# A graph network of four layers on one core: the feed-forward's transpose and the row of f go over DRAM, the relation check to ScalarE

## The chip, the core and the metric

The kernel runs on one core of a Trainium2 chip. Its time is the device time of one execution in microseconds (us). The profile is of one further execution, with its own time.

The engines are PE (TensorE, matrix products; PEld is its loading of weights, which overlaps the products), DVE (VectorE), ACT (ScalarE), POOL (GpSimd) and SP (SyncE, which here only issues transfers). Each engine works through its own list of instructions in order and waits on semaphores for the others. Products go to PSUM, which has eight banks of 2 KB per partition; everything else lies in SBUF, with 128 partitions, or in DRAM.

## The reference: what is computed

There are 64 graphs of 256 nodes with 256 features (x) and a 256 × 256 matrix of integers (adj), all in 32-bit floats. Four layers follow each other, and after each x becomes layernorm(x + layer(x)):

```python
# layer 0: attention with 8 heads where an edge goes one way or the other, then a feed-forward
x1 = layernorm(x + softmax(mask(q @ k.T / sqrt(32))) @ v @ Wo.T + bo)
ff = relu(x1 @ W1.T + b1) @ W2.T + b2
layer0 = layernorm(x1 + ff)
# layers 1 and 2: graph attention ("GAT"), e[i, j] = leaky_relu(f[i] + g[j]) where adj > 0
h = x @ W; f = h @ a[0]; g = h @ a[1]
layer1 = softmax(e) @ h + bias
layer2 = elu(softmax(e) @ h)
# layer 3: two convolutions over the relation adj == 1 (the other relation is always empty here)
conv(h) = elu(h @ w_root + b + (adj == 1).T @ h / degree @ w_rel[1])
layer3 = conv2(conv1(x))
```

In layer 3 both masks are made from the same adj: one is (adj == 1) and (adj != 1), which holds nowhere, so that only one relation is computed. The kernel checks such assumptions as it goes along and keeps the findings (`seen_sum`, `seen_inv`, `seen_fg`, `seen_rel`); a general version of the computation stands behind a branch at the end, and is entered only where one of them does not hold.

## The kernel before, in words

**Graphs.** `graph(g)` (from L653) describes the work on one graph as a list of operations for a planner, each on one engine and with its cost, the tiles that it reads and writes, and a function that issues the instructions. The operations of all 64 graphs go into one plan, so that the engines work on several graphs at a time.

**The order.** `Plan.schedule` (L197) lays all operations out in time before anything is issued: an engine that is free takes, among the operations that are ready and for whose tiles a buffer is free, the one with the earliest due date. The due date is the sum of a date for the kind of operation (`DUE`) and one for the graph (`LATER`). Both are lists of numbers found by a search. `RINGS`, `DRAM` and `SMALL` give the number of buffers of each kind of tile. A transfer has a cost, its time on the issuing queue, and a lag until its data are there (`SENT` 3.2 and `BACK` 5.5 for the bounce described below). An operation with the port mark "uses" is a VectorE operation with which the planner lets no POOL operation marked "waits" overlap. The result is a fixed order on each engine.

**Turning a tile.** A product needs the left operand with the features on the partitions, so each tile of 256 nodes × 256 features is turned before it is multiplied. There are three ways in the kernel:

- `transposed` (L691): four PE transposes (products with the identity) of 128 × 128 into one bank, and a ScalarE copy (L701) to the tile `T`.
- `bounced` (L714): one VectorE instruction turns all blocks of 32 × 32 (L719), four SP transfers write the result, 128 B a piece, to a DRAM tile `rows` (L723), one SP transfer reads it back as `T` (L726). The features come back in another order on the partitions (feature 128k + 32b + c on partition 4c + b), and the weights that are multiplied with them are loaded in that order by `spread` (L594).
- `rearranged` (L704): `bounced` for all but the last five graphs (`QUICK`); for those a ScalarE copy (L709) puts the features in the other order, and `transposed` turns the copy.

The GAT layers and the convolutions use `rearranged`. The feed-forward (L888) uses `transposed` for all graphs, and its W1 lies in plain order; the gain of the layer norm before it is multiplied into W1 at the start (L650, with the column `gcol`), its bias goes through W1 into b1 (L644, with `bcol`). The input of layer 0 has a way of its own (`input_transposed`, L730: eight transfers per graph and one VectorE instruction).

**A GAT layer** (`gat`, L912): four products with the weights give h and, in two more columns, f and g, and VectorE or ScalarE moves them to SBUF. Then f, which lies in one column of h, is needed as a row on every partition. PE makes it with two transposes of a column repeated 128 times, into the bank `pf` (L932). For each half VectorE adds pf, the column of g and the mask (L937); the leaky slope (L940), the exponential on ScalarE (L942) and the products with h (L945) follow.

**The relation** (`relation`, L977): VectorE makes rel = (adj == 1) at L981, and at L982 sums up (adj != 1) × rel, which must be zero, into a column of `seen_rel`.

**At the start** `setup` loads the weights on SP (W1 with one transfer of 1 MB at L602), and POOL loads the rows and columns of biases; `gcol` and `bcol` are two of those loads (L385).

Of the kernel before, what the change touches and what calls it, by code (L numbers as in the profile page):

```python
# [9 lines left out]
F32 = mybir.dt.float32  # L10
# [3 lines left out]
AF = mybir.ActivationFunctionType  # L14
ALU = mybir.AluOpType
# [3 lines left out]
P = 128  # L19
# [8 lines left out]
SENT, BACK = 3.2, 5.5  # L28


RINGS = {"x": 3, "adj": 4, "bits": 2, "am": 2, "gm": 6, "T": 4, "qk": 2, "v": 2, "p": 12, "both": 4, "inv": 1, "ctxT": 2, "X": 8,
         "xr": 1, "hid": 1, "h": 3, "e": 3, "n": 1, "rel": 3, "hi": 2, "lo": 2, "o": 4, "blocks": 1, "turned": 1, "xT": 2}
DRAM = {"rows": 6}
# [1285 lines left out]
```

## Time and profile before

| | |
|---|---|
| three runs | 2799.07 to 2801.94 us, median 2801.02 |
| profiled execution, its own time | 2798.13 us |
| its span | 2796.4 us |
| instructions in the span | 50418 |
| PE busy | 2762.3 us (99%), 16262 products recorded |
| PEld busy | 2128.1 us (76%) |
| DVE busy | 2486.5 us (89%), 6475 instructions |
| ACT busy | 1568.0 us (56%) |
| POOL busy | 855.0 us (31%) |
| moved by DMA | 284.08 MB, mean 102 GB/s |
| DMA packets | 808319, of them 651088 under 512 B |

The span runs from the first to the last recorded instruction, and the device time is 1.7 us longer. A product of 32-bit floats is recorded as two matmuls, a transpose and a product of the relation's type (fp32r) as one. In groups of instructions, a line reads: line of the kernel, engine, operation, output tile <- input tiles, shapes, count, then the busy time in us and the mean duration of one in ns, then how long the engine was idle just before them and what ended that. A line of the code can be that of a helper: all plain products stand under L747. The profile takes matmuls as pipelined, so that the recorded length of one reaches into the next, and the length of one is not the time that it takes from PE. In the transfers, the three figures are the count, the size of one, and the median time from issue to landing in us.

### The profile page before, as it was taken

What the parts mean: (1) busy time and instruction counts of PE and PEld (TensorE: products, weight loads), DVE (VectorE), ACT (ScalarE), POOL (GpSimd) and SP (SyncE); (2) the same over time, 40 slices, a digit from 0 to 9 for tenths busy, and PEclk for the clock granted to TensorE, in tenths of its full rate; (3) what the DMA queues carried; (4) which work ended last, traced back from release to release, by engine and by line L of the source; (5) the groups of instructions that cost most, each with busy time, mean ns of one, the idle gap of its engine ahead of it and who ended that gap; (6) DMA issues with size and microseconds to landing.
All of it is one profiled execution on the core that took longest, in us unless ns stands there. A gap on an engine that the chain in (4) does not pass through costs nothing. (4 is left out here: it accounts for less than half of the span.)

```text
span 2796.4 us, 50418 instructions
## 1 busy us (share of the span) xinstructions
PE 2762.3 (99%) x16262; PEld 2128.1 (76%) x16262; DVE 2486.5 (89%) x6475; ACT 1568.0 (56%) x3753; POOL 855.0 (31%) x1747
## 2 busy tenths in 40 slices
PE   7999999999999999999999999999999999999998
PEld 5787777777777777777777777777777777777774
DVE  5789999898998998998989989989989889899877
ACT  3555565555555555655555555556556555556466
POOL 2223233233232332332332322323323323223232
PEclk9999999999999999999999999999999999999999
DMA  7346455554545555554545556455555545544121
GB/s 188 78 88 125 88 122 104 105 107 103 113 97 107 111 102 102 112 105 102 108 104 110 99 106 118 95 102 113 103 102 110 105 95 108 104 97 103 42 50 32
DMA packets 808319, 284.08 MB, mean 102 GB/s; under 512 B 651088, under 2 KB 769104, under 8 KB 808048
## 3 DMA queue, kind: packets, MB, share of 16 engines
q1 hardware_dynamic: 763680, 229.77, 37.1%
q0 software_dynamic: 44368, 51.01, 12.3%
q8 instruction: 131, 2.15, 0.3%
q14 instruction: 140, 1.15, 0.1%
HBM read 152.19 MB, written 78.64 MB: 83 GB/s over the span
## 5 line engine op out<-in xcount | busy, mean ns | idle before, releaser
L761 POOL TENSOR_SCALAR rstd<-mv 128x2 f32<-128x2 f32 x384 | 116.4, 303 | 1359.4 <-DVE mv L758 1226.0
L747 PE MATMUL bank<-T,w 128*128 128x256 f32 x2048 | 475.4, 380 | 0.1
L747 PE MATMUL bank<-cw,T 128*128 128x512 f32 x1024 | 465.5, 594 | 0.3 <-ACT T L701 0.2
L747 PE MATMUL bank<-w,hid 128*128 128x256 f32 x2048 | 462.3, 379 | 0.0
L768 ACT ACTIVATE X<-X,rstd 128x256 f32<-128x256 f32 x640 | 349.4, 598 | 154.6 <-POOL rstd L764 151.2
L747 PEld LDWEIGHTS bank<-w,hid 128*128 128x128 f32 x2048 | 384.2, 190 | 53.6 <-issue 3.3
L747 PEld LDWEIGHTS bank<-T,w 128*128 128x128 f32 x2048 | 379.9, 190 | 54.8 <-issue 4.8
L847 ACT ACTIVATE p<-bank 128x512 f32<-128x512 f32 x512 | 302.1, 606 | 78.1 <-PE bank L841 78.1
L849 DVE TENSOR_TENSOR p<-p,am 128x512 f32<-128x512 f32 x512 | 331.9, 678 | 7.6 <-ACT p L847 7.4
L747 PEld LDWEIGHTS bank<-cw,T 128*128 128x128 f32 x1024 | 189.1, 190 | 181.0 <-issue 173.5
L762 POOL TENSOR_TENSOR rstd<-rstd,neghalf 128x2 f32<-128x2 f32 x384 | 310.8, 809 | 32.0
L873 DVE RECIPROCAL inv<-bank 128x256 f32<-128x256 f32 x128 | 219.5, 1743 | 110.6 <-PE bank L867 110.6
L902 ACT ACTIVATE hid<-bank,col_b 128x256 f32<-128x256 f32 x512 | 213.5, 468 | 106.9 <-PE bank L747 106.6
L747 PE MATMUL bank<-xT,wqkv 128*128 128x256 f32 x1024 | 238.6, 382 | 14.5 <-DMA wqkv<-in_WqkvT_dram 14.5
L747 PE MATMUL bank<-h,e 128*128 128x259 f32 x1024 | 252.0, 386 | 0.1
L747 PE MATMUL bank<-gw,T 128*128 128x258 f32 x1024 | 246.0, 381 | 0.0
L747 PEld LDWEIGHTS bank<-h,e 128*128 128x128 f32 x1024 | 189.3, 190 | 68.7 <-issue 43.2
L756 DVE BATCH_NORM_STATS2 st<-X 128x6 f32<-128x256 f32 x640 | 237.3, 412 | 4.2
L747 PEld LDWEIGHTS bank<-xT,wqkv 128*128 128x128 f32 x1024 | 193.8, 191 | 44.4 <-DVE row_b L414 14.5
L747 PEld LDWEIGHTS bank<-gw,T 128*128 128x128 f32 x1024 | 189.6, 189 | 29.9 <-issue 3.0
L965 ACT ACTIVATE n<-bank,r 128x256 f32<-128x256 f32 x128 | 60.6, 474 | 239.6 <-DVE X L970 149.2
L999 ACT CAST hi<-bank 128x256 fp32r<-128x256 f32 x256 | 98.7, 386 | 167.1 <-PE bank L747 166.5
(126 smaller groups left out, 4871.5 us busy)
## 6 DMA issues: line engine op xcount, KB each, us to landing
rows<-turned SPq DMA_DIRECT2D x944, 64.0 KB, 2.3
T<-rows SPq DMA_DIRECT2D x236, 256.0 KB, 2.8
adj<-in_adj_dram SPq DMA_DIRECT2D x128, 256.0 KB, 3.5
blocks<-in_x_dram SPq DMA_DIRECT2D x512, 32.0 KB, 2.4
xr<-in_x_dram SPq DMA_DIRECT2D x64, 256.0 KB, 2.9
x<-in_x_dram SPq DMA_DIRECT2D x64, 256.0 KB, 2.9
xr<-row_ln_b POOLq DMA_DIRECT2D x64, 256.0 KB, 5.1
x<-row_bo POOLq DMA_DIRECT2D x64, 256.0 KB, 4.7
```

Of the source, the lines that this page charges most:

```text
L747: nc.tensor.matmul(dst, lhsT=lhs(c), rhs=rhs(c), start=(c == 0), stop=(c == n - 1))
L756: nc.vector.bn_stats(stat()[:, i, :], y()[:, i, :])
L761: nc.gpsimd.tensor_scalar(rstd()[:, 0, :], mv()[:, :, 1], 1.0, EPS, op0=ALU.mult, op1=ALU.add)
L762: nc.gpsimd.tensor_tensor(rstd()[:, 0, :], rstd()[:, 0, :], neghalf[:, 0:NB], op=ALU.pow)
L768: nc.scalar.activation(y()[:, i, :], y()[:, i, :], AF.Identity, bias=rstd()[:, 1, i : i + 1], scale=rstd()[:, 0, i : i + 1])
L847: act(0.58, lambda pr=pr, k=k, sr=s[r]: nc.scalar.activation(pr(), sr(), AF.Exp, accum_out=seen_sum[:, k : k + 1]), [s[r]], [pr])
L849: dve(0.60, lambda pr=pr, kt=kt: nc.vector.tensor_tensor(pr(), pr(), am()[:, kt, None, :].to_broadcast([P, KB, N]), op=ALU.mult), [pr, am] ...
L873: dve(1.62, lambda hg=hg, pc=pc: nc.vector.reciprocal(inv()[:, hg, :], pc()[:, 1, :]), [pc], [(inv, hg)])
L902: act(0.36, lambda f=f, k=k, ph=ph: nc.scalar.activation(hid()[:, f + k, :], ph()[:, k, :], AF.Relu, bias=b1[:, f + k : f + k + 1]), [ph, ...
L965: act(0.36, lambda: nc.scalar.activation(n(), po()[:, 0:D], AF.Exp, scale=r()), [po, r], [n])
L999: act(0.27, lambda i=i, po=po: nc.scalar.copy(hi()[:, i, 0:D], po()[:, D:]), [po], [(hi, i)])
```

## The change

1. The feed-forward turns its tile by `rearranged` in place of `transposed`: over DRAM for 59 graphs, by a ScalarE copy and PE for the last five. W1 is loaded by `spread` with four transfers, and `gcol` and `bcol` by four small transfers each (`cols_spread`), in the same order of features. In products with w1, x1T is read as `xT()[:, kb::KB, :]`, two runs of 128 numbers.
2. `f_on_all` is new: for 59 graphs a VectorE instruction turns the column of f, repeated 32 times, in blocks into `cols`; an SP transfer writes partitions 0, 32, 64 and 96 of it as one row of 256 numbers (1 KB) to DRAM, and a second reads the row to all 128 partitions as `pf`, now a tile in SBUF. The additions of pf get the port mark "uses". The last five graphs keep the PE transposes.
3. The check of the relation becomes a ScalarE instruction: the sum of (rel − 0.5)², which is a quarter for each element that is 0 or 1. At the very end that known sum is subtracted and the rest squared.
4. The rings get `cols` (2), `pf` (3), `row` (6, in DRAM), and `rows` grows from 6 to 8. All numbers of `DUE` and most of `LATER` are new.
5. The general version reloads W1 in plain order and multiplies the gain in again.

```diff
+SENT_ROW, BACK_ROW = 2.6, 4.0
...
-         "xr": 1, "hid": 1, "h": 3, "e": 3, "n": 1, "rel": 3, "hi": 2, "lo": 2, "o": 4, "blocks": 1, "turned": 1, "xT": 2}
-DRAM = {"rows": 6}
+         "xr": 1, "hid": 1, "h": 3, "e": 3, "n": 1, "rel": 3, "hi": 2, "lo": 2, "o": 4, "blocks": 1, "turned": 1, "xT": 2, "cols": 2, "pf": 3}
+DRAM = {"rows": 8, "row": 6}
...
+    def cols_spread(name):
+        w = const.tile([P, KB], F32, tag=f"spread_{name}", name=f"spread_{name}")
+        view = t[name].rearrange("(k b c) -> b c k", b=4, c=32)
+        for b in range(4):
+            nc.gpsimd.dma_start(w[b::4], view[b])
+        return w
...
-    gcol, bcol = cols("ln1_g", KB), cols("ln1_b", KB)
+    gcol, bcol = cols_spread("ln1_g"), cols_spread("ln1_b")
...
-            load(c_w1, w1, "W1T")
+            spread(c_w1, w1, "W1T")
...
-                return xT, lambda kb, i: xT()[:, KB * i + kb, :]
+                return xT, lambda kb, i: xT()[:, kb::KB, :] if i is None else xT()[:, KB * i + kb, :]
...
-                x1T = transposed(x1)
+                x1T, x1T_at = rearranged(x1)
...
-                            lambda kb: x1T()[:, kb, :], KB), [x1T, c_w1], [ph], [hid])
+                            lambda kb: x1T_at(kb, None), KB), [x1T, c_w1], [ph], [hid])
...
+            def f_on_all(h, e):
+                if g < B - QUICK:
+                    cols, row, pf = new("cols", [P, NB, 32]), new("row", [1, NB * P]), new("pf", [P, N])
+                    dve(0.13, lambda: nc.vector.transpose(cols().rearrange("p i c -> p (i c)"),
+                                                          h()[:, :, F_COL : F_COL + 1].to_broadcast([P, NB, 32])),
+                        [(h, 0), (h, 1)], [cols], "uses")
+                    op("SP", 0.45, lambda: nc.sync.dma_start(row().rearrange("o (i b c) -> (o b) i c", i=NB, b=4), cols()[::32]),
+                       [cols], [row], lag=SENT_ROW)
+                    op("SP", 0.45, lambda: nc.sync.dma_start(pf(), row().to_broadcast([P, N])), [row], [pf], lag=BACK_ROW)
+                    return pf, "uses"
...
-                pe("spread", 0.18, spread, [(h, 0), (h, 1)], [pf], [e])
+                pf, port = f_on_all(h, e)
                 for i in range(NB):
                     dve(0.39, lambda i=i: nc.vector.scalar_tensor_tensor(e()[:, i, :], pf(), h()[:, i, G_COL : G_COL + 1],
                                                                          gm()[:, i, :], op0=ALU.add, op1=ALU.min),
-                        [pf, (h, i), gm], [(e, i)])
+                        [pf, (h, i), gm], [(e, i)], port)
...
-                dve(0.60, lambda: nc.vector.scalar_tensor_tensor(
-                    other(), adj(), 1.0, rel().bitcast(F32), op0=ALU.not_equal, op1=ALU.mult,
-                    accum_out=seen_rel[:, g : g + 1]), [adj, rel], [other], "uses")
+                act(0.62, lambda: nc.scalar.activation(other(), rel().bitcast(F32), AF.Square, bias=half[:, 0:1],
+                                                       accum_out=seen_rel[:, g : g + 1]), [rel], [other])
...
+    nc.vector.tensor_scalar(seen_rel, seen_rel, -0.25 * NB * N, None, op0=ALU.add)
+    nc.vector.tensor_tensor(seen_rel, seen_rel, seen_rel, op=ALU.mult)
```

More of the change, by code (lines that the diff above doesn't have):

```diff
@@ L409, in tile_gnn_stack @@
     minus = filled([P, 1], F32, "minus", -1.0)
+    half = filled([P, 1], F32, "half", -0.5)
     neghalf = filled([P, NT], F32, "neghalf", -0.5)
-    gcol, bcol = cols("ln1_g", KB), cols("ln1_b", KB)
+    gcol, bcol = cols_spread("ln1_g"), cols_spread("ln1_b")
     bq = const.tile([P, KB], F32, tag="bq", name="bq")
@@ L711, in rearranged @@
                 xT = transposed(spread)
-                return xT, lambda kb, i: xT()[:, kb, i * P : (i + 1) * P]
+                return xT, lambda kb, i: xT()[:, kb, :] if i is None else xT()[:, kb, i * P : (i + 1) * P]
             def bounced(xt):
@@ L910, in feed_forward, with spread @@
                 return y
+            def f_on_all(h, e):
[8 more added lines that the diff above has]
+                    return pf, "uses"
+                pf = new("bank", [P, N])
+                def spread():
+                    for i in range(NB):
+                        nc.tensor.transpose(pf()[:, i * P : (i + 1) * P],
+                                            h()[:, i, F_COL : F_COL + 1].to_broadcast([P, P]), ident)
+                pe("spread", 0.18, spread, [(h, 0), (h, 1)], [pf], [e])
+                return pf, None
             def gat(xt, layer, gm, seen, bias, finish):
@@ L927, in gat @@
                                                           h()[:, :, F_COL : G_COL + 1], op=ALU.mult), [(h, 0), (h, 1)], [], "uses")
-                pf = new("bank", [P, N])
-                def spread():
-                    for i in range(NB):
-                        nc.tensor.transpose(pf()[:, i * P : (i + 1) * P],
-                                            h()[:, i, F_COL : F_COL + 1].to_broadcast([P, P]), ident)
-                pe("spread", 0.18, spread, [(h, 0), (h, 1)], [pf], [e])
+                pf, port = f_on_all(h, e)
                 for i in range(NB):
@@ L1250, in tile_gnn_stack @@
             nc.vector.tensor_copy(eye[:, h, h * P : (h + 1) * P], ident_b)
+        g_col = gen.sb([P, KB], F32, "g_col")
+        nc.scalar.dma_start(g_col, t["ln1_g"].rearrange("(c p) -> p c", p=P))
+        nc.scalar.dma_start(w1, t["W1T"].rearrange("(c p) n -> p c n", p=P))
+        for c in range(KB):
+            nc.vector.tensor_scalar(w1[:, c, :], w1[:, c, :], g_col[:, c : c + 1], None, op0=ALU.mult)
         w_rel0 = []
```

95 rows, old and new, of tables (DUE, LATER) are left out of this document.

## Prediction

> **What bounds the kernel now.** I read first the table of stretches, which gives each engine's busy time in a stretch of the span (PE, PEld, DVE, ACT, POOL, then granted clock, DMA share, GB/s).
>
> ```profile
> 0.00:50.00 50.00, 31.70 (x233) 25.37 (x233) 24.46 (x57) 14.23 (x38) 16.56 (x29) 0.93 0.79 196
> 50.00:400.00 350.00, 349.94 (x2116) 272.25 (x2116) 306.95 (x773) 191.51 (x474) 101.27 (x208) 1.00 0.50 103
> 400.00:800.00 400.00, 400.00 (x2345) 309.03 (x2345) 366.27 (x951) 226.14 (x547) 126.28 (x249) 1.00 0.53 106
> ...
> 2720.00:2760.00 40.00, 38.06 (x163) 25.39 (x162) 35.76 (x122) 32.59 (x62) 9.10 (x25) 1.00 0.04 8
> 2760.00:2797.00 37.00, 23.00 (x94) 13.12 (x92) 23.07 (x75) 21.42 (x39) 9.52 (x22) 0.86 0.19 52
> ```
>
> From 50 to 2720 us PE has no gap; it idles 18.3 us at the start and some 16 us at the end. But a matmul's recorded duration overlaps the next one, so "busy" alone proves nothing. I therefore took PE's own timeline near the middle, where the first column is the start, the second the length.
>
> ```profile
> 1404.84 3.61 PE L747 MATMUL bank<-w,hid 128*128 128x256 f32 x16
> 1408.29 0.38 PE L932 MATMUL bank<-ident,h 128*128 128x128 f32 x2
> 1408.51 3.62 PE L747 MATMUL bank<-w,hid 128*128 128x256 f32 x16
> ...
> 1424.70 0.61 PE L698 MATMUL bank<-ident,X 128*128 128x128 f32 x4
> 1425.14 5.32 PE L747 MATMUL bank<-cw,T 128*128 128x512 f32 x12
> ```
>
> Sixteen matmuls take 1408.29 − 1404.84 = 3.45 us, 0.216 us from start to start; those of one form are alike all through the middle (the median start-to-start of the 2048 from L747 on w and hid is 0.216, the tenth and ninetieth percentiles 0.215 and 0.216). So PE issues at its own pace and waits for nobody: whatever leaves PE between 50 and 2700 us leaves the span, as long as nothing new makes PE wait. The groups that the change touches (count, then busy us and mean ns):
>
> ```profile
> L719 DVE STREAM_TRANSPOSE turned<-X 128x512 f32<-128x512 f32 x177 | 124.6, 704 | 9.9 <-ACT X L768 7.5 <-ACT hid L902 0.7
> L937 DVE SCALAR_TENSOR_TENSOR e<-bank,h,gm 128x256 f32<-128x256 f32 x256 | 116.2, 470 | 4.6 <-PE bank L932 4.6
> L968 DVE SCALAR_TENSOR_TENSOR n<-n,X 128x256 f32<-128x256 f32 x128 | 52.9, 413 | 2.3 <-ACT n L965 2.3
> L701 ACT COPY T<-bank 128x512 f32<-128x512 f32 x84 | 51.1, 609 | 9.4 <-PE bank L698 9.1
> L932 PE MATMUL bank<-ident,h 128*128 128x128 f32 x256 | 49.0, 273 | 0.0
> L982 DVE SCALAR_TENSOR_TENSOR e<-adj,rel 128x512 f32<-128x512 int32 x64 | 43.6, 681 | 0.1
> L876 ACT ACTIVATE inv<-inv 128x512 f32<-128x512 f32 x64 | 40.3, 630 | 43.6 <-DVE ctxT L874 33.4 <-DVE r L947 4.5
> L698 PE MATMUL bank<-ident,X 128*128 128x128 f32 x256 | 38.8, 274 | 0.0
> ```
>
> **The change, part by part.** *PE.* In 59 of the 64 graphs (all but the QUICK five) the feed-forward loses four transposes, and each of the two GAT layers two. Their price is not their 274 ns but the slot they take: 1425.14 − 1424.70 = 0.44 us for four, 1408.51 − 1408.29 = 0.22 us for two. 59 × 0.44 + 118 × 0.22 = 26.0 + 26.0 = **−52 us**. The last five graphs keep four transposes in the feed-forward, now of a spread copy. [...]
>
> One product is fed differently: the 2048 matmuls with w1 read x1T in two runs of 128 numbers instead of one of 256. No row shows this on that operand. A gain has no ground; the nearest rows are the transposes of L932, which read a column repeated 128 times, and of L698, which read plain columns: 273 and 274 ns, the same slot. I take nothing; the other end is 3% of 1888 × 0.216 us, 12 us, by the spread of the group means of one shape (379 to 391 ns).
>
> *DVE*, busy 2486 us. 59 block transposes × 0.704 = +41.5; the check of the relation goes, 64 × (0.681 + 0.081 for its accumulator) = −48.8. The e addition reads pf from SBUF: between 0.470 (L937, one bank) and 0.413 (L968, SBUF only), 236 × −0.05 = −12, bounds −13 and 0. The new transpose of 64 columns lies between 0.06 (a memset of two columns) and 0.704 (512 columns); 64/512 of 0.704 plus 0.06 is 0.15, nearest to the short one: +18, bounds +7 and +83. Sum −1, bounds −14 and +76: 2485 us of a span near 2750 is 90%, 93% at worst. DVE's waits hide it; the largest is `inv` at L873 waiting 110.6 us for PE. *ACT*, 56% busy: 59 copies × 0.609 = −36, 64 checks × (0.630 + 0.188, L876's row and its accumulator) = +52, five spread copies × 1.107 = +5.5. All beside PE.
>
> *Queues.* SP has some 1000 us of issue work now (944 row writes × 0.63, 512 block loads × 0.45, 236 reads × 0.35, 320 loads and stores × 0.39). It gains 236 × 0.63 + 59 × 0.35 + 236 × 0.45 = 276 us: 37% becomes 47%. The DMA engines stand at 0.53 in the middle; a quarter more bouncing and 118 reads of 128 KB bring at most 0.62. [...]
>
> ```profile
> rows<-turned SPq DMA_DIRECT2D x944, 64.0 KB, 2.3
> T<-rows SPq DMA_DIRECT2D x236, 256.0 KB, 2.8
> ...
> gw<-ga SPq DMA_DIRECT2D x8, 0.5 KB, 1.8
> ```
>
> *The two added waits.* (1) f over DRAM: eviction 0.42 (L923), transpose 0.15, write 1.8 (the 0.5 KB row), read 2.8 (twice its size), two additions 0.94, L940's 0.68, exp 0.63: 7.4 us, 8.0 with the long transpose. I laid the slots of this trace along the PE order of the built changed program. Between a GAT layer's last product and its first product with e stand 11.6 us of other PE work at least and 15.8 at the median (4.7 and 9.2 in the order of before). The cover holds by 3.6 to 8 us. On SP the read of the row waits for its write to land; up to nine transfers stand between the two, in 22 of 118 cases none, and then bounces, loads and the next graph's blocks are held about 1.8 us behind it. On DVE 6 to 31 instructions (median 18) stand between the transpose and the addition that needs pf; behind it wait mostly the multiplications by the mask, and PE's values behind those. (2) The feed-forward over DRAM: addition 0.69, statistics 1.05, POOL 1.6, scaling 1.1, transpose 0.70, four issues 2.5, landing 2.3, read 3.15: 13.1 us, against 23.0 us of PE work at least (median 36.7) between the wo product and w1. Covered.
>
> *The ends.* At the start PE waits until 14.51 for wqkv. In the new SP order one quarter of W1 (256 KB) goes ahead of it; at the 188 GB/s of the first slice that is 1.4 us, plus 0.6 of issue: **+2**. Six more column loads on POOL (0.73 each) fall in its 7.2 us wait for `row_bo`. At the end the last graph's feed-forward needs a spread copy, 1.107 us on its chain: **+1**. Between −1 and +6 for both.
>
> *Sum* against the profiled execution's own time, 2798.1 (span 2796.4 and 1.7 around it): −52 + 3 = 2749. It lies 2.9 below the median of the three runs, so I add 3: **2752**. New due dates also re-order every engine; PE's switches between tilings cost the same table of slots within 2 us (54 instead of 52 us saved over the whole order), left out of the sum.
>
> **The rivals.** *Stalls eat a part.* The PE order has tighter places too: between a conv product and the first product with its rest (lo), 183 pairs have under 2.5 us, against 74 before. For it: PE had no slack waits to lose. Against: pairs under 1.8 us are as many as before (16 and 15). At 0.3 us of stall per graph, or w1 read slower, it gives 2763 to 2790. *Slower.* The row trip through SP in order: where a row's write or read stands behind a bounce that itself waits (SP waited 406.7 us for L756 in 48 times, 9.7 at most), 7.4 us becomes 17. From an average stall of 52/118 = 0.44 us per GAT layer on, nothing is gained; at 1 us the time is 2752 + 118 = 2870. So 2805 to 2870. Against it: the margin above. *It does nothing:* DVE, 91% busy, takes the pace, its waits cannot shrink, and the time stays near 2796. Against: 34 us of its 400 are idle, and the change adds none. *More:* the starts overlap better, under 2741.
>
> **Chances.** 2741 to 2763: 0.72. Partly eaten: 0.14. Same pace by DVE: 0.04. Slower: 0.07. Over 52 us: 0.03. A measurement of this kernel tells about 0.2%, 5.6 us, from no change. Faster 0.72 + 0.14 + 0.03 and half of the DVE case make 0.91, same 0.02, slower 0.07. The range 2741 to 2776 leaves out the larger stalls and the slow case.
>
> **What would show it.** PE: some 15790 matmuls instead of 16262, the transposes of h down to 20, and still 400.00 busy in the middle stretches with more matmuls in each; DVE near 92 to 93% there; ACT's `T` copies 25. Wrong would be: gaps of PE ahead of products with e (f's trip), ahead of w1 (the feed-forward's trip), w1 slots above 0.216, or a start idle well over 20 us.

## The result, and the profile after

The changed kernel takes 2804.55 us at the median (2801.43 to 2812.56) where the kernel before takes 2799.69 on the same chip: a ratio of 1.0019, with a 95% interval of 1.0012 to 1.0026. The forecast was 2752, the range ended at 2776. So the change costs some 5 us where 48 were to be gained.

What the change was to remove is gone. The page of the profile after:

```profile
span 2806.6 us, 50451 instructions
...
PE 2744.8 (98%) x15790; PEld 2082.0 (74%) x15790; DVE 2480.0 (88%) x6527; ACT 1580.3 (56%) x3827; POOL 851.8 (30%) x1753
```

PE has 472 matmuls less, VectorE is no busier than before (2486.5), and the span is 10 us longer: engines that do less and end later have waited. The table of stretches says where (PE, PEld, DVE, ACT, POOL busy, then clock, DMA share, GB/s):

```profile
0.00:50.00 50.00, 29.68 (x201) 22.39 (x201) 23.37 (x54) 12.82 (x34) 18.38 (x31) 0.93 0.88 214
50.00:400.00 350.00, 347.33 (x2129) 270.89 (x2128) 304.81 (x757) 193.73 (x489) 102.01 (x207) 1.00 0.58 119
400.00:800.00 400.00, 394.11 (x2257) 296.95 (x2250) 361.06 (x945) 222.82 (x548) 123.34 (x248) 1.00 0.59 120
...
1200.00:1600.00 400.00, 393.32 (x2264) 295.75 (x2266) 359.70 (x946) 221.89 (x543) 127.46 (x249) 1.00 0.61 124
```

Before, PE had 400.00 of 400 in the middle (399.90 from 2000 to 2400) and 2345 to 2384 matmuls in a stretch; now 393 to 398, and 2257 to 2312. VectorE's busy time fell with it in most stretches, from 366 to 361 between 400 and 800. When both of the fullest engines get less done, look for something that each waits for. The groups of the changed operations show it (count, busy us and mean ns, then the idle time just before them and what ended it):

```profile
L730 DVE STREAM_TRANSPOSE turned<-X 128x512 f32<-128x512 f32 x236 | 165.3, 700 | 65.5 <-DMA rows<-turned 52.2 <-ACT X L779 8.1 <-issue 3.1
L962 DVE SCALAR_TENSOR_TENSOR e<-pf,h,gm 128x256 f32<-128x256 f32 x236 | 105.5, 472 | 16.7 <-DMA pf<-row 16.6
...
L1007 ACT ACTIVATE e<-rel,half 128x512 f32<-128x512 f32 x64 | 45.6, 713 | 4.1 <-DVE rel L1006 4.0
L927 DVE STREAM_TRANSPOSE cols<-h 128x64 f32<-128x64 f32 x118 | 28.0, 237 | 3.2 <-ACT h L953 3.1
```

The first line is the one that matters. Before, VectorE was idle 9.9 us ahead of its transposes of X, and it waited for the tile to turn. Now it is idle 65.5 us, and 52.2 of them (56.5 in 48 times with the transposes of o) end with `DMA rows<-turned`: the instruction waits until an earlier bounce's writes have read the buffer `turned` empty, and there is one such buffer. In the table of waits (us in total, times, longest) this is one row:

```profile
DVE turned L730 <- DMA rows<-turned: 56.5, 48, 4.6
```

PE feels it behind VectorE: its own gaps ahead of products with e, lo and hi sum to 19.5 us here, and to 7.2 in run 1 below, where the wait for the buffer is gone. The timeline (start, length, engine, line, what) shows one case:

```profile
499.70 0.67 DVE L730 STREAM_TRANSPOSE turned<-o 128x512 f32<-128x512 f32 x1
...
500.95 3.82 SPq L734 DMA_DIRECT2D rows<-turned  x4
...
505.48 2.94 SPq L748 DMA_DIRECT2D blocks<-in_x_dram  x6
506.98 0.71 DVE L730 STREAM_TRANSPOSE turned<-X 128x512 f32<-128x512 f32 x1 [0.38 <-DMA rows<-turned]
...
508.52 0.39 SPq L737 DMA_DIRECT2D T<-rows  x1
508.96 0.43 SPq L748 DMA_DIRECT2D blocks<-in_x_dram  x1
509.49 3.46 SPq L734 DMA_DIRECT2D rows<-turned  x4
...
515.88 0.71 DVE L730 STREAM_TRANSPOSE turned<-X 128x512 f32<-128x512 f32 x1 [4.47 <-DMA rows<-turned]
```

The transpose of 506.98 fills the buffer at 507.7. SP issues its writes only from 509.49, because it first reads back the bounce before (508.52) and loads blocks; the four issues take 3.46 us, and the next transpose, whose wait ends when they have landed, starts at 515.88. So the buffer was held 8.9 us, and VectorE stood for 4.47 of them with everything behind that transpose on its list. In the starts of all block transposes the distance from one to the next was under 8 us in 68 of 235 cases before; now it is in 172 of 294. That is not only because a fifth bounce was added: of the 172, 59 have a feed-forward tile as one of the two, and 113, out of 180 such pairs, are between two tiles that were bounced before the change too. So in the new order the old four stand closer together.

### The profile page after: what moved, and what is told of

The parts are those of the page before. It is cut to its first block, busy times and chain, and to the rows that moved or that the text cites. A ratio compares the mean times of both kernels' runs of the same rounds, so it can differ in the third digit from the quotient of the medians.

```text
span 2806.6 us, 50451 instructions
## 1 busy us (share of the span) xinstructions
PE 2744.8 (98%) x15790; PEld 2082.0 (74%) x15790; DVE 2480.0 (88%) x6527; ACT 1580.3 (56%) x3827; POOL 851.8 (30%) x1753
## 2 busy tenths in 40 slices
DMA packets 960073, 330.62 MB, mean 118 GB/s; under 512 B 780184, under 2 KB 913304, under 8 KB 959800
## 4 chain that ended last, share of the span: by engine, by line
PE 65%; DVE 18%; DMA 8%; SPq 3%; ACT 3%; issue 2%; POOL 1%; DVEq 0%; POOLq 0%; ACTq 0%
PE bank L758 55%; DMA rows<-turned 3%; PE bank L852 3%; PE bank L878 3%; PE bank L1036 3%; SPq L734 2%; DMA o<-X 2%; PE bank L873 2%; DVE turned L730 2%; DVE p L860 2%; DMA pf<-row 1%; DVE inv L884 1%; DVE st L767 1%; DVE X L689 1%; DVE lo L1024 1%
## 5 line engine op out<-in xcount | busy, mean ns | idle before, releaser
L772 POOL TENSOR_SCALAR rstd<-mv 128x2 f32<-128x2 f32 x384 | 102.0, 266 | 1434.4 <-DVE mv L769 1098.2
L758 PE MATMUL bank<-T,w 128*128 128x256 f32 x2048 | 464.4, 380 | 0.8 <-DMA T<-rows 0.6
L773 POOL TENSOR_TENSOR rstd<-rstd,neghalf 128x2 f32<-128x2 f32 x384 | 301.6, 785 | 32.1
L758 PE MATMUL bank<-xT,wqkv 128*128 128x256 f32 x1024 | 245.2, 386 | 7.8 <-DMA wqkv<-in_WqkvT_dram 7.1
L730 DVE STREAM_TRANSPOSE turned<-X 128x512 f32<-128x512 f32 x236 | 165.3, 700 | 65.5 <-DMA rows<-turned 52.2
```

Of the source, the lines that this page charges most:

```text
L730: dve(0.63, lambda: nc.vector.transpose(turned().rearrange("p b q n -> p (b q n)"), xt().rearrange("p i (k b c) -> p b (i k) c", k=KB, b=4 ...
L758: nc.tensor.matmul(dst, lhsT=lhs(c), rhs=rhs(c), start=(c == 0), stop=(c == n - 1))
L772: nc.gpsimd.tensor_scalar(rstd()[:, 0, :], mv()[:, :, 1], 1.0, EPS, op0=ALU.mult, op1=ALU.add)
L773: nc.gpsimd.tensor_tensor(rstd()[:, 0, :], rstd()[:, 0, :], neghalf[:, 0:NB], op=ALU.pow)
```

## The experiments

Unless a diff says otherwise, each kernel keeps the changed kernel's order on every engine. Times of the kernel before beside them were 2799.9 to 2800.7.

**1. A second buffer.**

```diff
-    seen_sum = filled([P, 8 * B], F32, "seen_sum", 0.0)
+    seen_sum = filled([P, 8], F32, "seen_sum", 0.0)
...
-                        pr, k = p[kt, r], 8 * g + 4 * kt + r
+                        pr, k = p[kt, r], 4 * kt + r
...
-        for o in plan.schedule():
+        order, seen = plan.schedule(), set()
+        for o in order:
+            for x in o.tiles:
+                if x.ring == "turned" and x not in seen:
+                    x.slot = len(seen) % 2
+                    seen.add(x)
+        for o in order:
             o.issue()
```

> The order of every engine is that of the changed kernel; only the tile that the block transposes write (turned) has two buffers in place of one, taken in turn. To make room, the column sums of exp keep 8 columns in place of 512, so that the last graph alone is looked at by that check. Theory A (the one buffer: the trace of the changed kernel has DVE idle 56.5 us ahead of 48 block transposes until the row writes of the transpose before have landed, and PE starves behind it): most of those 56 us go, the drift of PE in the middle falls by 30 to 45 us, 2760 to 2775. Rival B (the new order itself, its switches between tilings and tight pairs): not below 2795. Rival C (the row trip of f: DVE waits 16.6 us for pf): not below 2790.

Measured 2774.15 (2773.5 to 2775.37), ratio 0.9903 (0.9887 to 0.9920): 30 us less than the changed kernel, with the same order and the same transfers, and within theory A. The waits are gone (the group of the transposes) and PE is nearly full again (one of the stretches):

```profile
L730 DVE STREAM_TRANSPOSE turned<-X 128x512 f32<-128x512 f32 x236 | 164.7, 698 | 9.0 <-ACT X L779 5.2 <-DMA xr<-in_x_dram 3.3
```
```profile
400.00:800.00 400.00, 398.91 (x2289) 302.31 (x2288) 368.18 (x974) 228.57 (x564) 122.69 (x253) 1.00 0.59 124
```

**2 to 4. The added transfers left out, one buffer.** In 2 the f row's two transfers go (e reads a constant tile), in 3 the five of the feed-forward bounce (w1 multiplies a constant tile), in 4 both. The VectorE instructions stay. Edit of 2:

```diff
-                    op("SP", 0.45, lambda: nc.sync.dma_start(row().rearrange("o (i b c) -> (o b) i c", i=NB, b=4), cols()[::32]),
-                       [cols], [row], lag=SENT_ROW)
-                    op("SP", 0.45, lambda: nc.sync.dma_start(pf(), row().to_broadcast([P, N])), [row], [pf], lag=BACK_ROW)
+                    op("SP", 0.45, lambda: None, [cols], [row], lag=SENT_ROW)
+                    op("SP", 0.45, lambda: None, [row], [pf], lag=BACK_ROW)
+                    pf.at = pf_still
...
```

> Same order as the changed kernel. The 236 transfers of the f row are left out, and the addition reads a constant tile in place of pf, so that e is computed from the wrong f. Theory A: SP gets 115 us of issue time back and DVE's 16.6 us of waiting for pf go, but the block transposes still wait for their one buffer: 2785 to 2797. Rival C (the row trip of f is the cause): 2750 to 2770. Rival B: no change beyond 5 us, 2799 to 2806.

> Same order as the changed kernel. The five transfers of the feed-forward's bounce are left out in 59 graphs and w1 is multiplied with a constant tile; the block transpose on DVE stays, the check of the exp sums looks at the last graph alone. Theory A: the buffer is free at once after each of these 59 transposes, and SP has 180 us less to issue: 2755 to 2775. Rival C: not below 2790. Rival B: not below 2795.

> Same order as the changed kernel, with neither the transfers of the f row nor those of the feed-forward's bounce (both products then read constant tiles; check of the exp sums on the last graph alone). Theory A with C beside it: only the order's own cost stays, that is the 52 us that leave PE against some 13 us of added switches between tilings and 6 us more at the start: 2760 to 2772. Rival B, the order itself: not below 2790, since no transfer is left that could hold it.

Measured 2797.06 (ratio 0.9991, 0.9981 to 1.0000), 2793.68 (0.9975, 0.9966 to 0.9985) and 2788.18 (0.9953, 0.9936 to 0.9970). Run 2 stands at the edge of what was expected, 3 and 4 missed it by 15 to 20 us. The reason stands in the waits, one row of each run:

```profile
DVE turned L731 <- DMA rows<-turned: 57.8, 50, 4.3
DVE turned L731 <- DMA rows<-turned: 43.3, 38, 4.5
DVE turned L732 <- DMA rows<-turned: 44.4, 32, 4.9
```

I had thought that the fifth bounce a graph is what fills the buffer; but the four old ones, which the new order puts closer together, fill it without it. The changed kernel's own trace says so too: 39 of its 48 waits, 48.9 of the 56.5 us, stand between two old tiles, with no feed-forward tile as the one that holds the buffer or the one that waits. Taking the new traffic away gives 16 us, taking the buffer's wait away gives 30.

**5. The control: the kernel before with two buffers.** The edit of run 1 in the kernel before.

> The kernel before, in its own order on every engine, with a second buffer for the block transposes of the bounces (used in turn) and the check's table of row sums cut to 8 columns to make room. Theory A (the single buffer costs the changed kernel some 26 us only because its new order brings two bounces close together): the kernel before waited 9.9 us in sum at these transposes, nearly all of it beside work of TensorE, so it gains next to nothing: 2795 to 2802 against 2799.7. Theory B (a second buffer is simply worth that much to any order): 2770 to 2785.

Measured 2800.15, ratio 0.9999 (0.9990 to 1.0009). The second buffer has no worth of its own: the old order with four bounces does not need it, and the shorter `seen_sum` gains nothing either.

**6 and 7. Two buffers, and the transfers left out as well.** Run 1 with the edit of 2, and with that of 4.

> The changed kernel in its own order with two buffers for the transposes (2774.2 when run before), and the f row's two transfers left out: the addition into e reads a constant tile of the same shape, so e's values are not the reference's; the small transpose on VectorE stays. Theory A (with the second buffer, the largest wait that is left is VectorE's for the f row at the addition into e, 17.8 us in sum by the trace, and 118 issues leave SP): 2756 to 2768. Theory B (that wait lies beside other work; what is left over the forecast are switches of TensorE and the start): 2770 to 2776. That the whole rest is this wait: below 2752.

> As the run with two buffers and the f row's transfers left out, and the five transfers of the feed-forward bounce left out too in the 59 graphs that have it: the products with w1 read a constant tile, so their values are not the reference's; the block transposes on VectorE stay. With no transfer of the change left, what remains over the pace of TensorE are, by theory A, the switches between kinds of matmul that the new order adds (13 us) and the later start (6 to 8): 2745 + 20, so 2758 to 2766. Theory B (the old bounces wait as well in the new order, so little changes against the run before it): 2766 to 2775. If switches and start cost nothing: 2742 to 2750.

Measured 2769.94 (0.9894, 0.9878 to 0.9911) and 2770.32 (0.9890, 0.9873 to 0.9906). Of the 17.8 us that VectorE waits for `pf` in run 1, the end feels some 4; the intervals of the two ratios overlap, so that the 4 are a hint and not a measurement. The bounce's transfers, once the buffer is there, cost nothing that these runs can tell. Both runs missed theory A's range, by 2 and by 4 us, and run 7 lies in theory B's: without any new transfer 18 us over the forecast remain. In run 6 PE has its 400.00 again in the stretches from 400 to 1200, so that few of these 18 us can be stalls of the middle:

```profile
400.00:800.00 400.00, 400.00 (x2327) 305.01 (x2320) 370.25 (x977) 229.98 (x570) 126.25 (x255) 1.00 0.57 118
```

**8. The relation check back on VectorE**, in run 1, at the place in the list that ScalarE's had.

```diff
-                act(0.62, lambda: nc.scalar.activation(other(), rel().bitcast(F32), AF.Square, bias=half[:, 0:1],
-                                                       accum_out=seen_rel[:, g : g + 1]), [rel], [other])
+                act(0.62, lambda: nc.vector.scalar_tensor_tensor(
+                    other(), adj(), 1.0, rel().bitcast(F32), op0=ALU.not_equal, op1=ALU.mult,
+                    accum_out=seen_rel[:, g : g + 1]), [adj, rel], [other])
...
-    nc.vector.tensor_scalar(seen_rel, seen_rel, -0.25 * NB * N, None, op0=ALU.add)
-    nc.vector.tensor_tensor(seen_rel, seen_rel, seen_rel, op=ALU.mult)
```

> The changed kernel in its own order with two buffers for the transposes (2774.2), and the relation check back on VectorE, at the place in the order that ScalarE's has: 64 instructions of some 0.6 us, 39 us, go back onto VectorE and leave ScalarE. Theory A (with two buffers VectorE has room, about 10% of the span, and pays most of it from idle time): 2774 to 2786. Theory B (VectorE sets the time in stretches of the new order, so that each instruction counts): 2800 to 2815. If ScalarE's extra load cost more than VectorE's: below 2772.

Measured 2836.70, ratio 1.0128 (1.0111 to 1.0145): 62 us more than run 1, beyond even theory B. The instructions and the stretches of this run:

```profile
L1007 DVE SCALAR_TENSOR_TENSOR e<-adj,rel 128x512 f32<-128x512 int32 x64 | 42.7, 669 | 0.1
L1007 DVE DVE_READ_ACCUMULATOR e<-adj,rel 128x1 f32 x64 | 5.3, 83 | 0.0
```
```profile
400.00:800.00 400.00, 397.47 (x2313) 300.77 (x2306) 372.00 (x985) 220.77 (x540) 125.64 (x253) 1.00 0.57 123
...
2600.00:2860.00 260.00, 194.63 (x898) 140.45 (x897) 155.11 (x466) 128.25 (x244) 56.40 (x134) 0.91 0.15 34
```

They are 48 us, not 39, with their accumulators. VectorE does not become fuller than 372 of 400, 93%, where run 1 had 362 to 368: in this order its idle tenth was not there to be filled. Why 62 and not 48 isn't settled. PE idles 17 us more than in run 1 between 50 and 2600; the rest falls into the end, where the last five graphs follow each other with little beside them, PE waits 13.0 us for the ScalarE copy of their tiles (0.9 in run 1), and the granted clock was 0.91 (0.98 in run 1). The place was chosen for ScalarE, so the run tells that this order has no room on VectorE at that place, not that none has.

**9 to 12. New dates.** Can an order be found in which the change earns its 48 us? The planner got durations from the traces, and its dates were searched anew: 9 with two buffers, 10 with one, 11 for the kernel before; 12 as 9, but judged under durations with a spread.

```diff
-         "xr": 1, "hid": 1, "h": 3, "e": 3, "n": 1, "rel": 3, "hi": 2, "lo": 2, "o": 4, "blocks": 1, "turned": 1, "xT": 2, "cols": 2, "pf": 3}
+         "xr": 1, "hid": 1, "h": 2, "e": 3, "n": 1, "rel": 3, "hi": 2, "lo": 2, "o": 4, "blocks": 1, "turned": 2, "xT": 2, "cols": 2, "pf": 3}
...
-                    op("SP", 0.62, lambda a=a: nc.sync.dma_start(
+                    op("SP", 0.68, lambda a=a: nc.sync.dma_start(
...
-                    dve(0.13, lambda: nc.vector.transpose(cols().rearrange("p i c -> p (i c)"),
+                    dve(0.24, lambda: nc.vector.transpose(cols().rearrange("p i c -> p (i c)"),
...
```

> The changed kernel with two buffers for the block transposes (and two instead of three for h, to make room), and with due dates searched once more, after the planner's costs were set to what the traces show: a row transfer's issue on SP 0.68 us instead of 0.62, an input block 0.54, the f row's first transfer 0.58, the small transpose 0.24, the switch from row or column tiling to other matmuls 0.2 and from column to row tiling 0.13. The whole computation is done. Theory A (what was lost against the forecast is the order's: one buffer, issues planned too short, switches and start): with an order searched for the measured durations the forecast's time comes back, 2745 to 2760. Theory B (the order's part ends with the second buffer, the rest is contention that no order escapes): 2768 to 2780.

> The changed kernel with its single buffer for the block transposes, and due dates searched once more with the same measured durations in the planner. The whole computation is done. Theory A (the single buffer hurts only because the order on record was searched with issues of 0.62 us and so lets bounces follow each other too closely): an order that knows the longer issues loses little, 2750 to 2775. Theory B (five bounces a graph through one buffer are too many for any order of these engines): 2790 to 2806.

> The control for the search: the kernel before, its operations unchanged, with due dates searched by the same means and for as long, with the same measured durations in the planner. The whole computation is done. Theory A (its old order already keeps TensorE at its pace, so dates have nothing to give): 2788 to 2802. Theory B (the new search is simply a better search, and would have lifted either kernel): 2740 to 2775.

> The changed kernel with two buffers for the block transposes and two for h, and with due dates searched a second time: the order is now judged under durations that vary as the traces show them (row issues of 0.63 or 0.82 us, landings and VectorE instructions with a spread), and with the first products held until their transfers have landed (14 to 24 us), which the search before did not know and lost some 7 us by. The whole computation is done. Theory A (the order of the earlier search lost against its plan because the plan had no spread and too early a start): 2757 to 2770, below the 2774 of the changed kernel's own order with two buffers. Theory B (what is left over the forecast is not the order's): 2772 to 2782.

Measured 2779.83 (0.9927, 0.9910 to 0.9944), 2793.15 (0.9976, 0.9966 to 0.9985), 2808.97 (1.0031, 1.0019 to 1.0044) and 2786.70 (0.9950, 0.9933 to 0.9966). All four of theory A's ranges were missed, each on the slow side; 9 and 10 lie in theory B's. With two buffers, the changed kernel's own order (run 1, 2774) stayed better than 9 and 12. One reason could be read for 9 to 11: the planner does not know POOL's loads at the start, and the new dates put a product first that needs one of them. PE's timeline of run 9:

```profile
21.78 1.87 PE L582 MATMUL bank<-a,T 128*128 128x2 f32 x8 [21.78 <-DMA a<-in_a_dram]
...
25.36 1.06 PE L714 MATMUL bank<-xT,wqkv 128*128 128x256 f32 x2
```

The first product with wqkv starts at 25.4 instead of 18.2 (run 1). Run 12 did not cure it (20.2, behind a wait for `xT`) and waited elsewhere too. Runs 9 and 10 differ by 13 us, but in their dates and in the ring of h as well as in the buffer, so that the 13 can't be put down to the buffer alone. With one buffer in run 10 the distances under 8 us were 178, yet only 20.5 us of waits for the buffer were left, against 56.5: another order with five bounces waits less for the same single buffer, which again speaks for the order and against the mere number of bounces. Whether the forecast's time can be reached by dates stays open.

**13 and 14. A whole version, and its start.** Run 1 shortened a table that the checks need. Run 13 takes the room from the ring of T (three buffers) instead; 14 also lets SP issue wqkv ahead of the first quarter of W1.

```diff
...
+        first, quarter = plan.ops[0], plan.ops[2]
+        order.remove(first)
+        sp = [o for o in order if o.engine == "SP"]
+        order.remove(quarter)
+        order.insert(order.index(sp[9]) + 1, first)
+        order.insert(order.index(sp[14]) + 1, quarter)
...
```

> The changed kernel with its dates and order untouched and two buffers for the block transposes, the room for the second taken from the turned tiles T (three buffers instead of four) so that the whole computation with all its checks is done. Theory A (the second buffer is worth some 30 us, the fourth T buffer a few): 2774 to 2782. Theory B (the fourth T buffer was what held the bounces apart from their readers): above 2790.

> The kernel of the run beside it, and at the start SP issues wqkv ahead of the first quarter of W1, which goes behind wo. In the changed kernel PE waits for wqkv until 18.2 us, 3.7 us later than before the change. Theory A (the start's lateness goes straight into the end, since PE has no slack behind it): 2 to 5 us less than the run beside it. Theory B (what the start loses is made up behind it, or other transfers take the place of W1's quarter): the same within 1.5 us.

Measured 2779.44 (2774.88 to 2780.43; ratio 0.9922, 0.9908 to 0.9935) and 2777.37 (2776.91 to 2779.41; 0.9921, 0.9907 to 0.9934). Run 13 confirms the buffer: 25 us less than the changed kernel with one buffer of T less. In 14 PE's first product with wqkv starts at 17.02 instead of 18.93, and the median falls by 2.1, but the runs overlap and the two ratios are the same within their intervals: inconclusive. Runs 9, 13 and 14 lie within 3 us of each other, 20 to 23 us below the kernel before; 2774 would need the 2 KB of run 1 found where they cost nothing.

## Why the prediction was wrong, point by point

The sum went 52 us wrong (2804.5 against 2752). Some 49 of them are found, 34 by runs and 15 read from the slots in the traces without a run that tests them:

| term of the sum | forecast | found | from |
|---|---|---|---|
| waits for the one `turned` buffer | 0 | +30 | run 1 against the changed kernel, 5 |
| f row's trip | 0, covered | some +4 | run 6 against 1, intervals overlap |
| feed-forward trip | 0, covered | 0 | run 7 against 6 |
| PE's switches | within 2 | +11 | slots of the trace, not tested |
| start | +2 | +6 | PE's slots in 0 to 50 us (first product with wqkv at 18.3 instead of 14.5), not settled by run 14 |

- **The step that failed:** the forecast put VectorE's waits at nothing. "DVE's waits hide it", it says of VectorE's sum with its 59 added block transposes; I priced the instruction (0.704, measured 0.700) and left out what it needs: a buffer that stays taken until four writes have landed. By the forecast's own figures (transpose 0.7, issues 2.5, landing 2.3) a user holds it some 5.5 us, 1620 us of the span for 295 users; in the timeline above it was 8.9. The diff shows `rows`, `cols`, `pf` and `row` growing, and not `turned`. What the runs showed in place of the zero is 56.5 us of waits on VectorE, worth 30 us of the time (run 1). The cover that I worked out for the feed-forward's trip, 23.0 us of PE's work against 13.1, was right (run 7); but it was PE's view, and the wait falls on VectorE, which works in order and hands its lateness to `lo`, `e` and PE.
- **The dates are the other half of that step.** "New due dates also re-order every engine" stands in the forecast, and beyond the switches of PE nothing was counted for it. The count of users, 236 before and 295 now, does not explain the wait by itself: without the fifth bounce's transfers 43 of the 56 us are still there (run 3), and 48.9 of the 56.5 stand between two old tiles. The old order does not need the second buffer (run 5); the new one does, and in it the old bounces stand closer together. Whether any order with a fifth block transpose on VectorE's list must set them so close is not shown; run 10's, with one buffer, waited 20.5 us.
- **PE's saving** was right in kind: 15790 matmuls, 20 transposes of h, 25 copies to `T`, as forecast, and w1's slots stayed at 0.216 (median) with its operand in two runs. The switches were wrong: PE changes its tiling 357 times now, 290 before. I had laid a table of slots from the old order along the new one. Where the old order had next to no example, the table fell back on the ordinary slot: the masks' transposes right after a row product (34 times now, 2 before) start 0.204 us later than the table had it, products of hi (19) and of q and k (16) after one of p and v 0.138, hi after q and k 0.202 (6). That is 13.0 us, less 1.9 of the same kind before, all of it read from the traces: no run changes the switches alone.
- **VectorE's small terms:** the addition of pf from SBUF takes 472 ns where 420 was assumed (470 from PSUM before): no gain. The 64-column transpose takes 237 ns instead of 150. Both together are 22 us of VectorE, which the total hides (2480 against 2485 forecast).
- **ScalarE's check** was right, 0.713 and 0.188 instead of 0.630 and 0.188, beside PE. Run 8 shows what I did not say: with it back on VectorE, at that place, this order takes 62 us more.
- **The rivals.** "Slower" (2805 to 2870) came nearest to the number, by luck, since its mechanism is wrong: its f row on SP costs some 4 us with the buffer there, 7 without, not 53 or more. "Stalls eat a part" saw PE's tight places (`lo`); PE does wait there (5.2 us, 0.8 in run 1), but as the last link behind VectorE, not as the cause. "DVE takes the pace" does not fit: VectorE had 361 of 400 where it had 366 before, and had become later without becoming fuller.

## What to carry to other kernels

When a change adds users to a ring or moves them, work out how long one user holds its buffer, from the instruction that takes it to the landing of the transfer that frees it, and compare that with the distance between neighbours on the engine's list, before and after, the closest ones first: a ring of one that caused no wait can be the new bound, and no busy column showed it here. The total (users times holding time) says little, since the waits came from neighbours that had moved together. Treat a new order as an edit of its own: give the old order the new buffer, and the new order the old work, before crediting either. And judge an order found by search against a table of durations by runs: the four searched here came out 7 to 20 us above what was expected of them.

## What else the runs showed of the hardware

- SP's issue of one row write (512 pieces of 128 B) takes 0.79 us on the mean where it overlaps the 3 us from the start of a POOL issue (312 of 1180 after), and 0.63 elsewhere (before: 0.84 for 310 of 944, and 0.64). The median is 0.63 in both, so the long issues make the difference: 77 of the 312 take over 0.8 us, and 27 of the other 868. The planner has 0.62 for all.
- VectorE's busy share in the stretches from 400 to 2400 us was 90 to 93% before, after and in runs 1 to 4, 6 to 8 and 12 to 14 (358.8 to 372.0 of 400), and 48 us of added work (run 8) raised it by only 2 to 4 us in each 400 and lengthened the run by 62.
- A fifth more packets, 960073 against 808319, raised the DMA share in the middle from 0.51 to 0.53 up to 0.59 to 0.62. With the buffer there, the feed-forward's part of them cost the end no time (run 7 against 6, where the share is 0.49 to 0.52 against 0.55 to 0.58).
